# Two float32r passes in place of three bfloat16 passes for a feed-forward product, and V's columns packed

## The chip, the cores and the metric

The kernel runs on one core of a Trainium2 chip. The metric is device time in microseconds (us) for one execution, lower is better. The engines are named as in the profile: PE is TensorE's matmul (PEld its weight loads), DVE is VectorE, ACT is ScalarE, POOL is GpSimd, SP is the engine that issues the DMAs.

## The reference

Four sublayers in a row act on x of 16 batches × 256 tokens × 256 features in float32. After each one, its output is added to its input and a layer norm follows:

```python
x = layernorm(x + L0_attn(x))   # 16 heads; Fourier transform of q and kv per head, cumulative sum over tokens
x = layernorm(x + L0_ffn(x))    # gate over 8 experts, the best expert's low-rank update
x = layernorm(x + L1_attn(x))   # softmax attention, 16 heads of 16 features
x = layernorm(x + L1_ffn(x))
```

The change concerns the last two. In the last one the weights are ternary: each group of 64 is replaced by −1, 0 or 1 times a bfloat16 scale.

```python
w1 = ternary(W_fc)                       # 1024 x 256
h = square(relu(x @ w1.T))               # the product that is changed
h = h * rsqrt(mean(h*h) + eps)
out = h @ ternary(W_proj).T
```

In softmax attention, each head's 256 tokens × 16 features of V are multiplied by the exponentials of the scores. The sum of the exponentials comes from a column of ones beside V's 16 columns.

## The kernel before, in words

**Order of the work.** The kernel writes down operations with engines, planned costs, inputs, outputs and priorities. `Order.run` then goes through a planned time, picks at each step the operation that can start first (among those within a small slack, the one of the best priority) and emits it. The order on each engine is therefore fixed when the kernel is built, and it follows from the planned costs: `pe([pb], [xs, (w1T, q)], 12 * 0.11, go)` is one such cost. Where an operation lists two ways, such as ACT or DVE, the planner takes the one that ends first.

**Stages.** The 16 batches go in 4 groups of 4. `front(b)` computes the first two sublayers of one batch. `attention(i)` computes softmax attention for group i: products for Q, K and V (L810), a first pass of scores (L864) whose row maxima DVE reduces (L873), a second pass (L898) that ACT exponentiates (L907), products with V (L913), and the output product (L955). `back(b)` computes the last sublayer of one batch. While attention of group i has priority, `back` of group i−1 and `front` of group i+1 fill in. The `back` of the last group comes after everything else.

**The last sublayer, `back`.** PE transposes x3 to put features on partitions (L977). x is then split into an exact sum of three bfloat16 terms in tile `xs`: ACT copies and rounds the first (L980), DVE subtracts it into `rest` (L981), ACT or DVE rounds the second (L983), DVE or POOL subtracts for the third (L988, L989). For each of four `q`, PE computes 256 rows of h as 2 × 6 matmuls of 256 columns (L1000): two feature halves by three terms. ACT takes relu (L1009), ACT or DVE squares it (L1012, L1013), ACT squares again for the mean (L1017), and DVE or POOL sums that over the hidden features (L1025). L1035 is the second product, in float32; L1044 sums the squares over partitions; L1054 scales and adds x3; a layer norm follows. There are two `xs` buffers, one `h`, one `sq` and twelve `work` buffers.

**Weights.** `ternary` computes w1T (bfloat16) and w2T (float32) once in SBUF, with an eviction from PSUM at the end (`evacuate`, L359 on ACT or L360 on DVE).

**V.** Tile `v` holds, for each of 32 blocks of 128 tokens and 4 batches, 32 columns: 16 features, one column of ones, 15 columns of zeros. POOL sets it up with two memsets (L425, L426), and for each group four DMAs (L835) write the 16 features of one batch each from DRAM. L913 takes the 32 columns as the stationary operand, and the 32 result rows of each batch go to one quarter of PSUM's partitions. L921 to L925 use only the first 17.

Of the kernel before, what the change touches and what calls it, by code (L numbers as in the profile page):

```python
# [9 lines left out]

F32 = mybir.dt.float32
BF16 = mybir.dt.bfloat16
AF = mybir.ActivationFunctionType
ALU = mybir.AluOpType
AX = mybir.AxisListType
# [2 lines left out]
P = 128  # L18
D = 256
S = 256  # L20
NB = 16
GB = 4
NG = NB // GB
H = 16
HD = 16
NE = 8
NR = 8
HID = 1024
# [112 lines left out]
class Order:  # L141
# [11 lines left out]
    def fixed(self, ap):  # L153

        t = Logical(None, None, None)
        t.slot = Slot(ap)
        return t
# [126 lines left out]
def forward(ctx, tc, x, xt, wq, wkv, wo0T, f0, degen, cs, wqkvT, wo1T, wfc, wproj, cst, out):  # L284
# [5 lines left out]
    order = Order(tc)  # L290
# [3 lines left out]
    def place(name, shape, dtype=F32):  # L294
        return sb.tile(shape, dtype, name=name)

    def const(name, shape):
        return fixed(place(name, shape))
# [29 lines left out]
        order.slot("wb", place(f"wb{i}", [P, 512], BF16))  # L328
        order.slot("sb", place(f"sb{i}", [P, 8], BF16))
    for i in range(2):  # L330
        order.slot("xs", place(f"xs{i}", [P, 3 * 512], BF16))
    order.slot("lane", *[None] * 4)
    order.limit = {("ps", "r"): 2, ("ps", "a"): 6, ("lane", "r"): 2}
    v = const("v", [P, 2 * H, GB, 32])

    order.slot("vd", *[dp.tile([GB, S - VT, NJ * HD], F32, name=f"vd{i}") for i in range(2)])
    o = const("o", [P, S // 32, D])
# [51 lines left out]
    dg = const("dg", [72, D])  # L389
    slope, center = const("slope", [P, NE]), const("center", [P, NE])  # L390
    wqr, wo1 = const("wqr", [P, 2, 3 * D]), const("wo1", [P, 2, D])
    w1T, w2T = fixed(place("w1T", [P, 2, HID], BF16)), const("w2T", [P, HID // P, D])
    a = lambda t: t.slot.ap

    order.prio = -10.0
# [26 lines left out]

    dve([ones], [], P, lambda: V.memset(a(ones), 1.0))
    dve([mhalf], [], 2, lambda: V.memset(a(mhalf), -0.5))
    pool([v], [], 3.6, lambda: G.memset(a(v), 0.0))  # L425
    pool([v], [], 0.3, lambda: G.memset(a(v)[:, :, :, HD : HD + 1], 1.0))  # L426

    def warm():

# [370 lines left out]
    def attention(i):  # L800
# [32 lines left out]
        for g in range(GB):  # L833
            op(
                (SP, 0.1, lambda g=g: nc.sync.dma_start(  # L835
                    a(v)[:, :, g, 0:HD],
                    vd.slot.ap[g].rearrange("t e -> (t e)")[2 * ZQ * HD - VT * NJ * HD :].rearrange("(n p d) -> p n d", p=P, d=HD),
                )),
                [(v, g)], [vd],
            )  # L840
# [10 lines left out]
        def part(g, rows, which, h, at=0, n=S):  # L851
            lo = which * ZQ + h * S + at
            return zt_[32 * g : 32 * g + rows, lo : lo + n]


        for hh in range(2):
# [32 lines left out]
        for hp in range(H // 2):  # L889
            av = ps([P, 2, S], "a")  # L890
            for hk in range(2):
                h = hp * 2 + hk
                sc = [ps([P, 2, S], "a") for _ in range(GB)]

                def go(sc=sc, h=h):
                    for c in range(2):
                        for g in range(GB):
                            T.matmul(  # L898
                                sc[g].v[:, c, :], part(g, HD + 1, 1, h, c * P, P), part(g, HD + 1, 0, h),
                                start=True, stop=True,  # L900
                            )

                pe(sc, [zq, zr[h // 8], v, turn], 0.95, go, mode="r")
                es = []
                for g in range(GB):
                    e = tile_("es", [P, 2, S])
                    act([e], [sc[g]], 512, lambda e=e, sc=sc, g=g: A.activation(e.v, sc[g].v, AF.Exp, scale=HD ** -0.5))  # L907
                    es.append(e)

                def go(es=es, av=av, h=h, hk=hk):  # L910
                    for c in range(2):
                        for g in range(GB):
                            T.matmul(  # L913
                                av.v[32 * g : 32 * g + 32, hk, :], a(v)[:, h * 2 + c, g, :], es[g].v[:, c, :],
                                start=(c == 0), stop=(c == 1),
                            )

                pe([(av, hk)], [*es, v, turn], 0.87, go, mode="c")

            ou, rc = tile_("work", [P, 2, S // 32, 32]), stat(2, S // 32)  # L920
            dve([ou], [av], 512, lambda ou=ou, av=av: V.transpose(ou.v.rearrange("p k u d -> p (k u d)"), av.v.rearrange("p k s -> p (k s)")))  # L921
            dve([rc], [ou], 80, lambda ou=ou, rc=rc: V.reciprocal(rc.v.unsqueeze(3), ou.v[:, :, :, HD : HD + 1]), us=0.22)
            dve(
                [(o, hp)], [ou, rc], 256,
                lambda ou=ou, rc=rc, hp=hp: V.tensor_tensor(  # L925
                    a(o)[:, :, ts(hp, 2 * HD)].rearrange("p u (k d) -> p k u d", d=HD),
                    ou.v[:, :, :, 0:HD],
                    rc.v.unsqueeze(3).to_broadcast([P, 2, S // 32, HD]),
                    ALU.mult,
                ),  # L930
                us=0.42,
            )
# [33 lines left out]
    def back(b, late):  # L966
# [1 line left out]
        kind = "p" if late else "r"  # L968
        x3 = x3s.pop(b)

        xs, rest = tile_("xs", [P, 3, 2, S]), tile_("work", [P, 2, S])
        bx = ps([P, 2, S], kind)

        def go():
            for t in range(2):
# [2 lines left out]

        pe([bx], [x3, small, terned], 0.43, go)
        act([(xs, 0)], [bx], 512, lambda: A.copy(xs.v[:, 0], bx.v))  # L980
        dve([rest], [bx, (xs, 0)], 512, lambda: V.tensor_tensor(rest.v, bx.v, xs.v[:, 0], ALU.subtract))  # L981
        op(
            [(ACT, 0.57, lambda: A.copy(xs.v[:, 1], rest.v)), (DVE, 0.6, lambda: V.tensor_copy(xs.v[:, 1], rest.v))],  # L983
            [(xs, 1)], [rest],
        )
        op(
            [
                (DVE, 0.7, lambda: V.tensor_tensor(xs.v[:, 2], rest.v, xs.v[:, 1], ALU.subtract)),  # L988
                (POOL, 1.3, lambda: G.tensor_tensor(xs.v[:, 2], rest.v, xs.v[:, 1], ALU.subtract)),  # L989
            ],  # L990
            [(xs, 2)], [rest, (xs, 1)],
        )
        h, sq, acc = tile_("h", [P, HID // P, S]), tile_("sq", [P, HID // P, S]), tile_("work", [P, S])
        for q in range(HID // P // 2):
            pb = ps([P, 2, S], kind)

            def go(pb=pb, q=q):
                for i in range(2):
                    for n in range(6):
                        T.matmul(  # L1000
                            pb.v[:, i, :], a(w1T)[:, n // 3, ts(q * 2 + i, P)], xs.v[:, n % 3, n // 3, :],
                            start=(n == 0), stop=(n == 5),
                        )

            pe([pb], [xs, (w1T, q)], 12 * 0.11, go)
            r = tile_("work", [P, 2, S])
            hq = lambda q=q: h.v[:, q * 2 : q * 2 + 2, :]

            act([r], [pb], 512, lambda pb=pb, r=r: A.activation(r.v, pb.v, AF.Relu))  # L1009
            op(  # L1010
                [
                    (ACT, 0.57, lambda r=r, hq=hq: A.activation(hq(), r.v, AF.Square)),  # L1012
                    (DVE, 0.73, lambda r=r, hq=hq: V.tensor_tensor(hq(), r.v, r.v, ALU.mult)),  # L1013
                ],
                [(h, q)], [r],
            )
            act([(sq, q)], [(h, q)], 512, lambda hq=hq, q=q: A.activation(sq.v[:, q * 2 : q * 2 + 2, :], hq(), AF.Square))  # L1017
# [114 lines left out]
```

## Time and profile before

| | us |
|---|---|
| three runs: median (lowest to highest) | 840.29 (838.42 to 840.89) |
| the profiled execution's own time | 840.28 |
| its span from first to last instruction | 838.3 |
| PE busy | 801.0 |
| DVE busy | 636.5 |
| ACT busy | 433.9 |
| POOL busy | 118.1 |
| L1000: 768 matmuls, busy | 95.9 |
| L1000's weight loads, busy | 75.9 |

All profile numbers come from one execution. A busy time is the union of the durations of instructions; matmuls are pipelined, so a matmul's duration (282 ns on average at L1000) is longer than the distance to the next one, and the distance is what counts for throughput. Weight loads (PEld) overlap the matmuls before them. The granted clock of TensorE was 0.944 on average. Where a line of the profile ends in brackets, it gives idle time ahead of the instruction and the instruction that ended it. "L1000" is line 1000 of the kernel before.

### The profile page before, as it was taken

The page shows a single profiled execution, that of the slowest core. Times are in us where ns is not written, and L with a number is a line of the kernel's source. Part 1 is how long each engine was busy: PE and PEld are TensorE (multiplying, and loading weights), DVE is VectorE, ACT ScalarE, POOL GpSimd, SP SyncE. Part 2 cuts the span into 40 slices and gives each one's busy share as a digit, 9 for nine tenths or more (in the row PEclk, how much of TensorE's full clock was granted, in tenths as well). Part 3 has the DMA queues.
Part 4 walks back from the last instruction along what each step waited for, and adds up shares of the span by engine and source line. Part 5 has one row for each costly group of instructions (what it writes and reads, how often), then busy time and mean ns, then how long its engine had stood idle before and what let it go on. Part 6 is the DMA issues. An engine that isn't in the chain of part 4 may idle for free.

```text
span 838.3 us, 15181 instructions
## 1 busy us (share of the span) xinstructions
PE 801.0 (96%) x5912; PEld 568.5 (68%) x5912; DVE 636.5 (76%) x1442; ACT 433.9 (52%) x858; POOL 118.1 (14%) x309
## 2 busy tenths in 40 slices
PE   9997799999989999998999999999999999999896
PEld 6775468765665676775666676776566678856785
DVE  2888799766778998866579899767668898644654
ACT  5745410268762444676562444875752425395652
POOL 1022000010131011012012001112120001101212
PEclk9998695699999999999799999999999899999998
DMA  8001025000000431011000440000000610000000
GB/s 297 18 24 39 0 46 67 14 15 26 28 13 2 76 49 27 14 39 39 5 23 1 75 51 15 27 26 11 4 1 20 81 13 27 14 15 1 2 26 25
DMA packets 86892, 27.17 MB, mean 32 GB/s; under 512 B 67932, under 2 KB 84132, under 8 KB 86820
## 3 DMA queue, kind: packets, MB, share of 16 engines
q1 hardware_dynamic: 86820, 26.20, 14.4%
q8 instruction: 46, 0.75, 0.4%
q14 instruction: 26, 0.21, 0.1%
HBM read 16.76 MB, written 8.91 MB: 31 GB/s over the span
## 4 chain that ended last, share of the span: by engine, by line
PE 83%; DVE 8%; ACT 5%; POOL 1%; issue 1%; DMA 1%; DVEq 0%; ACTq 0%; POOLq 0%
PE bank L1035 11%; PE bank L1000 10%; PE bank L810 10%; PE bank L864 10%; PE bank L913 8%; PE bank L898 8%; PE bank L598 6%; PE bank L955 3%; PE bank L697 3%; DVE nm L873 2%; PE bank L721 2%; PE bank L643 2%; PE bank L782 2%; PE bank L544 2%; DVE work L1025 1%
## 5 line engine op out<-in xcount | busy, mean ns | idle before, releaser
L907 ACT ACTIVATE zt<-bank 128x512 f32<-128x512 f32 x256 | 135.6, 609 | 79.4 <-PE bank L898 79.0
L873 DVE TENSOR_REDUCE nm<-bank 128x2 f32<-128x512 f32 x256 | 157.2, 680 | 13.3 <-PE bank L864 13.1
L1035 PE MATMUL bank<-w2T,h 128*128 128x256 f32 x512 | 118.5, 383 | 0.0
L1035 PEld LDWEIGHTS bank<-w2T,h 128*128 128x128 f32 x512 | 94.5, 190 | 17.2 <-issue 5.6
L864 PE MATMUL bank<-zt 16*128 16x256 f32 x1024 | 99.8, 457 | 0.5 <-DVE nm L873 0.4
L552 POOL TENSOR_SCALAR st<-st 128x2 f32<-128x2 f32 x80 | 17.0, 213 | 580.2 <-DVE st L560 387.0
L1000 PE MATMUL bank<-xs,w1T 128*128 128x256 bf16 x768 | 95.9, 282 | 1.7 <-DVE xs L988 0.8
L1000 PEld LDWEIGHTS <-w1T 128*128 128x128 bf16 x768 | 75.9, 101 | 21.8 <-issue 10.4
L810 PE MATMUL bank<-wqr,x2T 128*128 128x512 f32 (+1 forms) x256 | 87.7, 499 | 0.9 <-ACT x2T L359 0.9
L864 PEld LDWEIGHTS bank<-zt 16*128 16x128 f32 x1024 | 68.2, 209 | 25.1 <-DVE nm L873 10.8
L898 PE MATMUL bank<-zt 17*128 17x256 f32 x1024 | 81.9, 417 | 0.6 <-ACT zt L907 0.4
L913 PE MATMUL bank<-zt,v 128*32 128x256 f32 x1024 | 78.7, 393 | 1.1 <-ACT zt L907 1.0
L810 PEld LDWEIGHTS bank<-wqr,x2T 128*128 128x128 f32 x256 | 49.1, 195 | 36.5 <-issue 30.4
L898 PEld LDWEIGHTS bank<-zt 17*128 17x128 f32 x1024 | 53.4, 192 | 24.7 <-issue 15.7
L819 DVE STREAM_TRANSPOSE zt<-bank 128x1024 f32<-128x1024 f32 (+1 forms) x48 | 64.5, 1455 | 5.9 <-PE bank L810 5.0
L1025 DVE TENSOR_REDUCE work<-sq 128x256 f32<-128x2048 f32 x16 | 59.0, 3688 | 3.9 <-ACT sq L1017 3.9
L598 PE MATMUL bank<-wf,x 128*128 128x512 f32 x128 | 61.3, 611 | 0.0
L1009 ACT ACTIVATE work<-bank 128x512 f32<-128x512 f32 x64 | 38.1, 598 | 43.7 <-PE bank L1000 35.7
L553 POOL TENSOR_TENSOR st<-st,mhalf 128x2 f32<-128x2 f32 x80 | 57.4, 718 | 6.2
L913 PEld LDWEIGHTS bank<-zt,v 128*32 128x32 f32 x1024 | 32.1, 110 | 36.4 <-ACT zt L907 11.8
L359 ACT COPY work<-bank 128x512 f32<-128x512 f32 (+1 forms) x33 | 16.9, 511 | 69.5 <-PE bank L810 65.3
L558 DVE BATCH_NORM_STATS2 st<-work 128x6 f32<-128x256 f32 x116 | 43.1, 412 | 0.4
(204 smaller groups left out, 1135.1 us busy)
## 6 DMA issues: line engine op xcount, KB each, us to landing
x<-in_xT SPq DMA_DIRECT2D x16, 256.0 KB
v<-vd SPq DMA_DIRECT2D x16, 256.0 KB
out<-work SPq DMA_DIRECT2D x16, 256.0 KB
x<-in_x SPq DMA_DIRECT2D x12, 256.0 KB
vd<-work SPq DMA_DIRECT2D x12, 256.0 KB
vd<-work SPq DMA_DIRECT2D x12, 128.0 KB
h<-in_wfc SPq DMA_DIRECT2D x4, 256.0 KB
sq<-in_wproj SPq DMA_DIRECT2D x4, 256.0 KB
```

Of the source, the lines that this page charges most:

```text
L553: pool([dst], [dst, mhalf], 0.7, lambda: G.tensor_tensor(dst.v, dst.v, a(mhalf)[:, 0:n], ALU.pow))
L598: T.matmul(pb.v.rearrange("p a s k -> p (a s k)"), xT.v[:, c, ts(t, P)], a(wf)[:, c].rearrange("p a s f -> p (a s f)"), start=(c == 0), st ...
L810: T.matmul(b.v.rearrange("p j d -> p (j d)"), x2T.v[:, c, tb].rearrange("p g k -> p (g k)"), a(wqr)[:, c, j0 * HD : (j0 + nj) * HD], start ...
L819: lambda b=b, tb=tb, j0=j0, nj=nj: V.transpose(ztv[:, j0 : j0 + nj, ts(tb, 32)], b.v.unsqueeze(2).to_broadcast([P, nj, 2, HD])),
L864: T.matmul(sc[g].v[:, t, :], part(g, HD, 0, h, t * P, P), part(g, HD, 1, h), start=True, stop=True,)
L873: lambda nm=nm, sc=sc, g=g, h=h: V.tensor_reduce(nm.v[:, g, h % 8, :], sc[g].v, AX.X, ALU.max, negate=True),
L898: T.matmul(sc[g].v[:, c, :], part(g, HD + 1, 1, h, c * P, P), part(g, HD + 1, 0, h), start=True, stop=True,)
L907: act([e], [sc[g]], 512, lambda e=e, sc=sc, g=g: A.activation(e.v, sc[g].v, AF.Exp, scale=HD ** -0.5))
L913: T.matmul(av.v[32 * g : 32 * g + 32, hk, :], a(v)[:, h * 2 + c, g, :], es[g].v[:, c, :], start=(c == 0), stop=(c == 1),)
L1000: T.matmul(pb.v[:, i, :], a(w1T)[:, n // 3, ts(q * 2 + i, P)], xs.v[:, n % 3, n // 3, :], start=(n == 0), stop=(n == 5),)
L1025: (DVE, 2.2, lambda: V.tensor_reduce(acc.v, sq.v.rearrange("p k s -> p s k"), AX.X, ALU.add)),
L1035: T.matmul(pw.v[:, t, :], h.v[:, k, ts(t, P)], a(w2T)[:, k, :], start=(k == 0), stop=(k == HID // P - 1))
```

## The change

The first product of `back` gets x as a sum of two float32 terms[...] held as float32r, in place of three bfloat16 terms. w1T is kept as float32r too. ACT's copy (L980) rounds the first term, DVE's subtraction (L981) leaves the second, and the later cast and subtraction go. A group of one `q` has 2 × 4 matmuls in place of 2 × 6, and its planned cost goes from 12 × 0.11 to 8 × 0.11. `xs` takes 4 KB per partition and buffer in place of 3 KB, and w1T 8 KB in place of 4 KB.

V's blocks are packed to 17 columns: 16 features and the column of ones. The matmul still takes 32 columns, so 15 of them are the features and ones of the blocks behind, and rows 17 to 31 of the result, which nothing uses, are no longer zero. One memset to 1.0 sets up the whole tile. The tile has 15 columns at its end so that the last slice stays inside.

```diff
-        order.slot("xs", place(f"xs{i}", [P, 3 * 512], BF16))
+        order.slot("xs", place(f"xs{i}", [P, 2 * 512], F32R))
-    v = const("v", [P, 2 * H, GB, 32])
+    v = const("v", [P, 2 * H * GB * (HD + 1) + 31 - HD])
-    w1T, w2T = fixed(place("w1T", [P, 2, HID], BF16)), const("w2T", [P, HID // P, D])
+    w1T, w2T = fixed(place("w1T", [P, 2, HID], F32R)), const("w2T", [P, HID // P, D])
-    pool([v], [], 3.6, lambda: G.memset(a(v), 0.0))
-    pool([v], [], 0.3, lambda: G.memset(a(v)[:, :, :, HD : HD + 1], 1.0))
+    va = a(v)[:, 0 : 2 * H * GB * (HD + 1)].rearrange("p (n g d) -> p n g d", g=GB, d=HD + 1)
+    pool([v], [], 2.0, lambda: G.memset(a(v), 1.0))
...
-                    a(v)[:, :, g, 0:HD],
+                    va[:, :, g, 0:HD],
...
+        def v_part(g, n):
+            at = (n * GB + g) * (HD + 1)
+            return a(v)[:, at : at + 32]
...
-                                av.v[32 * g : 32 * g + 32, hk, :], a(v)[:, h * 2 + c, g, :], es[g].v[:, c, :],
+                                av.v[32 * g : 32 * g + 32, hk, :], v_part(g, h * 2 + c), es[g].v[:, c, :],
...
-        xs, rest = tile_("xs", [P, 3, 2, S]), tile_("work", [P, 2, S])
+        xs = tile_("xs", [P, 2, 2, S])
...
-        dve([rest], [bx, (xs, 0)], 512, lambda: V.tensor_tensor(rest.v, bx.v, xs.v[:, 0], ALU.subtract))
-        op(
-            [(ACT, 0.57, lambda: A.copy(xs.v[:, 1], rest.v)), (DVE, 0.6, lambda: V.tensor_copy(xs.v[:, 1], rest.v))],
-            [(xs, 1)], [rest],
-        )
-        op(
-            [
-                (DVE, 0.7, lambda: V.tensor_tensor(xs.v[:, 2], rest.v, xs.v[:, 1], ALU.subtract)),
-                (POOL, 1.3, lambda: G.tensor_tensor(xs.v[:, 2], rest.v, xs.v[:, 1], ALU.subtract)),
-            ],
-            [(xs, 2)], [rest, (xs, 1)],
-        )
+        dve([(xs, 1)], [bx, (xs, 0)], 512, lambda: V.tensor_tensor(xs.v[:, 1], bx.v, xs.v[:, 0].bitcast(F32), ALU.subtract))
...
-                    for n in range(6):
+                    for n in range(4):
                         T.matmul(
-                            pb.v[:, i, :], a(w1T)[:, n // 3, ts(q * 2 + i, P)], xs.v[:, n % 3, n // 3, :],
-                            start=(n == 0), stop=(n == 5),
+                            pb.v[:, i, :], a(w1T)[:, n // 2, ts(q * 2 + i, P)], xs.v[:, n % 2, n // 2, :],
+                            start=(n == 0), stop=(n == 3),
                         )
-            pe([pb], [xs, (w1T, q)], 12 * 0.11, go)
+            pe([pb], [xs, (w1T, q)], 8 * 0.11, go)
```

## The prediction

> **What bounds the kernel now.** I read the page's busy times first, then its chain of work that ended last. In the first line each engine has busy time, share of the span and instructions; in the second, each entry is a line of the kernel with its share of the chain.
>
> ```profile
> PE 801.0 (96%) x5912; PEld 568.5 (68%) x5912; DVE 636.5 (76%) x1442; ACT 433.9 (52%) x858; POOL 118.1 (14%) x309
> PE bank L1035 11%; PE bank L1000 10%; PE bank L810 10%; PE bank L864 10%; PE bank L913 8%; PE bank L898 8%; PE bank L598 6%; PE bank L955 3%; PE bank L697 3%; DVE nm L873 2%; PE bank L721 2%; PE bank L643 2%; PE bank L782 2%; PE bank L544 2%; DVE work L1025 1%
> ```
>
> PE carries the chain, and L1000, the product that the change rewrites, is 10% of it (some 87 us). But an average over stages hides where another engine is level with PE. So next I cut the run at the stages of batch groups 1 to 3 (columns: window, its length, busy time of PE, PEld, DVE, ACT, POOL, granted clock, DMA share, GB/s).
>
> ```profile
> 276.00:325.00 49.00, 48.94 (x429) 36.55 (x429) 47.16 (x76) 16.81 (x29) 2.19 (x6) 1.00 0.33 48
> 325.00:440.00 115.00, 109.58 (x906) 76.73 (x905) 82.47 (x242) 78.60 (x159) 19.35 (x55) 0.96 0.09 27
> 465.00:520.00 55.00, 54.84 (x463) 40.85 (x460) 52.79 (x90) 20.48 (x39) 4.64 (x14) 0.97 0.33 49
> 520.00:620.00 100.00, 98.62 (x846) 66.76 (x844) 70.88 (x204) 72.98 (x152) 15.94 (x44) 1.00 0.05 15
> 648.00:700.00 52.00, 51.93 (x409) 37.21 (x409) 46.93 (x70) 18.23 (x32) 2.06 (x3) 0.90 0.31 41
> 700.00:775.00 75.00, 74.33 (x759) 53.38 (x753) 40.31 (x84) 47.94 (x92) 11.35 (x30) 1.00 0.05 16
> 775.00:838.30 63.30, 52.62 (x353) 46.07 (x351) 36.14 (x62) 30.74 (x55) 12.65 (x34) 0.95 0.05 18
> ```
>
> Two kinds alternate. In 276–325, 465–520 and 648–700 (first score pass, row maxima L873 on DVE) PE and DVE are both full. In 325–440, 520–620 and 700–775 (second score pass, exponentials) PE alone is full. Narrowed to L1000, each of these six windows holds 96 of its 768 matmuls, and the tail from 775 us holds 192. The timeline of a first pass shows the balance (start, duration, engine, line).
>
> ```profile
> 280.76 1.49 PE L1000 MATMUL bank<-xs,w1T 128*128 128x256 bf16 x12
> 280.91 8.70 DVE L873 TENSOR_REDUCE nm<-bank 128x2 f32<-128x512 f32 x14 [1.03 <-PE bank L864]
> 282.17 0.74 PEld L864 LDWEIGHTS bank<-zt 16*128 16x128 f32 x16 [0.21 <-issue]
> ```
>
> PE alternates a score group and an L1000 group: L1000 starts at 280.76 and again at 283.25, a period of 2.49 us. DVE does four maxima in the same time, 8.70/14 × 4 = 2.49 us. Neither waits.
>
> **What the skill says, against this trace.** "FP8 and Floating Point Precision", TensorE Precision Notes: true float32 takes four passes through the array, while reduced-precision float32 reads the four bytes and truncates. The trace agrees with the four: on the chain 48 bf16 matmuls of 256 columns took 5.24 us, 109 ns each; a float32 product at L1035 is two records, 24 of which took 5.18 us, so 2 × 216 = 432 ns, four times as long. No float32r runs here. One pass for it is my reading of that note.
>
> "TensorE: Matmul & The Clock Gate", Weight-path perf modes: fast weight load works for 128 columns if the dtype isn't FP32. The rows agree that float32 loads are slower.
>
> ```profile
> L1035 PEld LDWEIGHTS bank<-w2T,h 128*128 128x128 f32 x512 | 94.5, 190 | 17.2 <-issue 5.6
> L1000 PEld LDWEIGHTS <-w1T 128*128 128x128 bf16 x768 | 75.9, 101 | 21.8 <-issue 10.4
> 299.22 0.55 PEld L1044 LDWEIGHTS bank<-ones,work 128*128 128x128 f32 x4
> 774.93 0.60 PE L977 MATMUL bank<-small,x 128*128 128x128 f32 x4
> ```
>
> A mean duration is latency, though; what counts is how closely loads follow each other. Four float32 loads with one-column matmuls (L1044) took 0.55 us, so (550 − 192)/3 = 119 ns apart. Four float32 transposes (L977), each with its own load, took 0.60 us with one of 273 ns at the end, so 109 ns apart. A float32-sized load therefore fits about the 109 ns that a 256-column pass takes; it isn't the 190 ns of the row.
>
> **The change, part by part.**
>
> *L1000, removed.* There are 16 batches × 4 = 64 groups; each goes from 12 matmuls to 8. At one pass and 109 ns a group falls from 1.31 to 0.87 us: 64 × 4 × 0.109 = 27.9 us of PE. The records that ran at half clock take about twice that, which I don't count. By place:
> - Second-pass windows: 32 matmuls off in each, 3.5 us × 3 = 10.5. PE idles there 5.4 of 115, 1.4 of 100 and 0.7 of 75 us, so nearly all is real: I take 9.4 (90%).
> - First-pass windows: also 10.5 on PE, but a shorter L1000 group leaves DVE's 2.49 us period standing. DVE idles only 49.00 − 47.16 = 1.8, 2.2 and 5.1 us there, and loses of its own two third-term subtractions, 2 × 0.68 = 1.4 us. Each window can give between 1.4 (DVE's loss) and 3.5 us, unless the planner moves other PE work in. I take 2.1 each, 6.3.
> - Tail: 192 matmuls, of which the chain holds 176 (46, 12, 36, 12, 24 and 46). A third of 176 × 0.109 is 6.4 us.
>
> *The split of x.* One float32r copy on ACT (L980, 0.59 us) and one subtraction on DVE (L981, 0.68) stay, with a float32-sized output. The cast L983 (13 on ACT at 0.61, 3 on DVE) and the third term L988 (14 on DVE at 0.68, 2 on POOL) go. Mostly they lie beside PE work. In the tail they are on the chain (start, duration, step):
>
> ```profile
> 815.94 0.61 DVE work L981
> 816.55 0.02 issue
> 816.57 0.63 ACT xs L983
> 817.20 0.02 issue
> 817.22 0.70 DVE xs L988
> ```
>
> The last batch's L1000 starts right behind, at 817.96: 0.63 + 0.70 = 1.3 us off. The first tail batch has the same pair at 778.48–779.72: 1.2 off. Together 2.5 us. What is late next there is PE itself with L1035. One work buffer per batch is freed as well, priced at nothing, since the longest waits name none.
>
> *Costs taken at nothing.* Writing float32r instead of bf16: a 128x512 ACT copy took 586–590 ns with either output. w1T's four evictions likewise. V's packing: one POOL memset of 2191 columns for two of 4096 and 128; by the first (3.51 us) some 1.9 us instead of 3.8, with V first used at 153.6 us. Stationary slices of V stay 32 contiguous columns; now 15 of them hold neighbours' values that nothing reads. The load (L913) starts at multiples of 68 bytes; its 110 ns load hides behind 256-column streams, bound +10% of those loads, none exposed.
>
> *V's DMA.* 16 transfers of 64-byte pieces, destination step 68 instead of 128 bytes. The skill ("DMA: Bandwidth & Descriptors", How a descriptor splits into AXI transactions) says that pieces not starting at 256-byte steps begin at the boundary below, which costs beats; so some pieces may cost more. No such pieces run here. Lower bound 0; upper bound twice: the DMA share is 0.73–0.78 over the 15 us of each group's transfer, so up to 11.7 us later. V lands at about 143, 300, 490 and 673 us; the second pass starts at 153.6, 325.3, 518.5 and 703.0. Cover of 11 us or more; doubled, group 0's row-maxima transfers, queued behind V on SP (landed by 144), would come 2 us late. I take 0.
>
> *Sum:* 9.4 + 6.3 + 6.4 + 2.5 = 24.6 us. The profiled run took 840.28 us (span 838.3 plus 2.0 around it), 0.01 from the median of 840.29. 840.3 − 24.6 = 815.7. No wait is added. The planner writes a new order of all work from the shorter costs; I allow ±6 us for where fillers now fall.
>
> **The rivals.**
>
> *A, slower: float32r isn't one pass.* If the array takes four-byte moving data at half rate, a matmul costs what one float32 record of 256 columns does, 216 ns. Float32 transposes of 128 columns take 109 ns, the price of 256 bf16 columns, which speaks for it; that transposes needn't be paced like products speaks against, as does the skill's note. Then L1000 costs 512 × 216 = 110.6 against 83.9 us: +26.7 us on PE, less 2.5 from the split: 864 us. It decides above 83.9/512 = 164 ns per matmul; at 140 ns, a float32 load's duration as a floor, half the gain stays: about 828.
>
> *B, DVE keeps the first passes.* One pass, but the first-pass windows give only 1.4 us each (4.2) and the tail's third-to-fourth gap absorbs half of its 8.9: 840.3 − 9.4 − 4.2 − 4.4 = 822. PE that waits more could also fall to half clock, as it did in 123–155 us (0.54 granted while DVE was full), which the skill (the same TensorE page, Part 1: The HAM clock gate) ascribes to idle windows of 3.4 us; two such windows would add about 3: 825.
>
> *C, more than the sum.* Before the last split, PE idles 808.7–817.9 while L1025 (3.7 us) holds DVE. A shorter split may be placed ahead of it: up to 6 us more, 809.
>
> **How the numbers follow.** One pass near the sum 0.50; B 0.25; C 0.10; A 0.15, of which the 140 ns middle case 0.02 and the slow one 0.13. The predicted time is the likeliest, 816. The first three cases lie in 803–830; the slow one's 864 would need a range that no case fills in between, so I stop at 834 and leave it out, with a little more for a worse order. The fast cases and the middle one hold 0.87; I give 0.03 of it to a worse order that eats the gain down to within 0.3% (2.5 us, about what a measurement of this kernel can tell from no change): faster 0.84, same 0.03, slower 0.13.
>
> **What would show it.** L1000 with 512 records of 108–120 ns from start to start, in groups of eight of about 0.9 us; PE busy about 770–775 us; no L983 or L988; second-pass windows shorter by 3 us each with PE still full; first-pass windows shorter by 1.4–3.5 us, DVE over 96% busy and PE with gaps. V landing at least 5 us before each second pass. The prediction is wrong if L1000's spacing is over 164 ns, if PE idles tens of us more at half clock, or if the second passes begin by waiting on V.

## The result: no change beyond the noise

| | us |
|---|---|
| before, median of 20 runs (lowest to highest) | 839.46 (838.15 to 840.89) |
| after, median of 20 runs (lowest to highest) | 839.17 (833.69 to 841.2) |
| ratio after to before, 95% interval | 0.9991 (0.998 to 1.0002) |
| the profiled execution after, and its span | 840.1, 838.3 |
| mean granted clock, before and after | 0.944, 0.92 |

The prediction said 816. The product got shorter, by rather less than it said; the larger part of the gain was lost elsewhere. In the kernel after, line numbers are a few off: L994 is the product (L1000 before), L985 and L986 are ACT's copy and DVE's subtraction of the split, L1029 is the second product (L1035), L869 the first pass of scores (L864), L878 its row maxima (L873), L903 the second pass (L898).

The page after, engine totals and chain, as shown for before:

```profile
PE 803.6 (96%) x5656; PEld 575.5 (69%) x5656; DVE 632.8 (75%) x1428; ACT 420.8 (50%) x842; POOL 114.7 (14%) x306
PE bank L1029 12%; PE bank L869 12%; PE bank L811 10%; PE bank L903 8%; PE bank L918 8%; PE bank L994 8%; PE bank L599 6%; DVE nm L878 3%; PE bank L698 3%; PE bank L960 2%; PE bank L722 2%; PE bank L644 2%; PE bank L783 2%; PE bank L545 2%; DVE st L559 1%; PE bank L662 1%
```

There are 256 matmuls fewer (5912 to 5656), and L994's share of the chain fell from 10% to 8%. Yet PE's busy time rose, from 801.0 to 803.6 us, and L869, which the change doesn't touch, went from 10% to 12%. The product itself is close to a single pass (first the chain: start, duration, step; then the groups by line and form: busy time, mean ns of one, idle time before):

```profile
339.43 2.83 PE bank L994 x24
```

```profile
L869 PE MATMUL bank<-zt 16*128 16x256 f32 x1024 | 117.3, 505 | 1.3 <-DVE nm L878 1.3
L994 PE MATMUL bank<-xs,w1T 128*128 128x256 f32 x512 | 72.5, 294 | 1.2 <-DVE xs L986 1.2
```

24 matmuls in 2.83 us are 118 ns each. From start to start inside a group, at full clock, the median step is 118 ns (363 of 372 steps lie between 115 and 122), against 109 for bfloat16. L869's busy time was 99.8 us before: 17.5 us more for the same 1024 matmuls.

In every trace here the granted clock is either 1.00 or 0.50, and a number between is the mean of a window. A stretch at 0.50 is called half clock below; most steps of the product took 213 ns in such stretches, in before as in after.

The windows of before, cut again (window, length, busy PE, PEld, DVE, ACT, POOL with counts, granted clock, DMA share, GB/s):

```profile
276.00:325.00 49.00, 48.29 (x366) 35.17 (x368) 44.08 (x74) 9.67 (x18) 3.10 (x8) 0.93 0.49 51
325.00:440.00 115.00, 111.48 (x904) 76.42 (x897) 85.22 (x239) 81.99 (x168) 19.82 (x56) 0.97 0.09 27
465.00:520.00 55.00, 54.70 (x406) 37.97 (x406) 49.89 (x87) 16.41 (x34) 4.80 (x11) 0.88 0.42 50
520.00:620.00 100.00, 98.71 (x813) 72.00 (x811) 71.16 (x195) 67.98 (x139) 17.71 (x46) 0.95 0.04 12
648.00:700.00 52.00, 52.00 (x359) 37.37 (x358) 47.27 (x75) 12.26 (x23) 2.20 (x6) 0.77 0.44 51
700.00:775.00 75.00, 74.11 (x733) 54.19 (x733) 36.14 (x63) 52.09 (x101) 6.96 (x18) 0.98 0.04 12
775.00:838.30 63.30, 53.93 (x322) 49.02 (x320) 39.11 (x72) 28.99 (x54) 14.89 (x40) 0.96 0.05 17
```

Read the first, third and fifth. PE is "busy" throughout, but with fewer matmuls than before (366, 406 and 359, where there were 429, 463 and 409) and at a lower clock (0.93, 0.88, 0.77 for 1.00, 0.97, 0.90). ACT shows the same: 9.67, 16.41 and 12.26 us for 16.81, 20.48 and 18.23. The fillers of `back` have left the first passes. The stage times, each from the first matmul of a kind to the first of the next, say where the time went:

| us against before | predicted | after |
|---|---|---|
| up to group 1's first QKV matmul | 0 | +1.6 |
| QKV to first second-pass score, groups 1 to 3 | −6.3 | +3.5 −3.2 −5.5 = −5.2 |
| first second-pass score to next QKV or output product | −9.4 | −7.2 +10.9 +7.0 = +10.7 |
| tail from the last group's output product | −8.9 | −7.1 |
| sum | −24.6 | 0.0 |

The second passes, where PE alone is full and 9.4 us were to be gained, got 10.7 longer: that is where the fillers went. The timeline of group 2's and group 3's first passes shows one step of how they were pushed out (start, duration, engine, line):

```profile
491.05 0.59 ACT L985 CAST xs<-bank 128x512 fp32r<-128x512 f32 x1 [0.18 <-PE bank L982]
...
493.24 2.46 DVE L878 TENSOR_REDUCE nm<-bank 128x2 f32<-128x512 f32 x4
...
515.34 0.66 DVE L986 TENSOR_TENSOR xs<-bank,xs 128x512 fp32r<-128x512 f32 x1
...
683.04 0.59 ACT L985 CAST xs<-bank 128x512 fp32r<-128x512 f32 x1 [3.21 <-PE bank L982]
...
698.37 0.68 DVE L986 TENSOR_TENSOR xs<-bank,xs 128x512 fp32r<-128x512 f32 x1
```

ACT rounded the first term at 491.05, and DVE subtracted at 515.34, 24.3 us later, with row maxima in between; in group 3 from 683.04 to 698.37, 15.3 us. The longest such distance in these passes before was 14.5 us. The L994 groups of that batch need the second term. So in group 2 one batch's product starts inside the first pass, and the next at 517.5, in the second pass, while before both started inside (473.6 and 496.5). In group 3 the second one starts at 699.4, 3.7 us before the first pass ends.

### The profile page after: what moved, and what is told of

Its sections match the earlier page's. It is cut to its first block, busy times and chain, and to the rows that moved or that the text cites. A ratio compares the mean times of both kernels' runs of the same rounds, so it can differ in the third digit from the quotient of the medians.

```text
span 838.3 us, 14648 instructions
## 1 busy us (share of the span) xinstructions
PE 803.6 (96%) x5656; PEld 575.5 (69%) x5656; DVE 632.8 (75%) x1428; ACT 420.8 (50%) x842; POOL 114.7 (14%) x306
## 4 chain that ended last, share of the span: by engine, by line
PE 83%; DVE 9%; ACT 5%; POOL 2%; issue 1%; DVEq 0%; ACTq 0%; POOLq 0%
PE bank L1029 12%; PE bank L869 12%; PE bank L811 10%; PE bank L903 8%; PE bank L918 8%; PE bank L994 8%; PE bank L599 6%; DVE nm L878 3%; PE bank L698 3%; PE bank L960 2%; PE bank L722 2%; PE bank L644 2%; PE bank L783 2%; PE bank L545 2%; DVE st L559 1%; PE bank L662 1%
## 5 line engine op out<-in xcount | busy, mean ns | idle before, releaser
L878 DVE TENSOR_REDUCE nm<-bank 128x2 f32<-128x512 f32 x256 | 157.3, 680 | 14.8 <-PE bank L869 14.4
L869 PE MATMUL bank<-zt 16*128 16x256 f32 x1024 | 117.3, 505 | 1.3 <-DVE nm L878 1.3
L1029 PE MATMUL bank<-w2T,h 128*128 128x256 f32 x512 | 118.1, 382 | 0.0
L1029 PEld LDWEIGHTS bank<-w2T,h 128*128 128x128 f32 x512 | 94.5, 190 | 16.4 <-issue 4.4
L869 PEld LDWEIGHTS bank<-zt 16*128 16x128 f32 x1024 | 81.9, 232 | 31.0 <-DVE nm L878 13.4
L903 PE MATMUL bank<-zt 17*128 17x256 f32 x1024 | 86.5, 422 | 1.8 <-ACT zt L912 1.6
L903 PEld LDWEIGHTS bank<-zt 17*128 17x128 f32 x1024 | 56.7, 195 | 25.8 <-issue 14.6
L994 PE MATMUL bank<-xs,w1T 128*128 128x256 f32 x512 | 72.5, 294 | 1.2 <-DVE xs L986 1.2
L994 PEld LDWEIGHTS bank<-xs,w1T 128*128 128x128 f32 x512 | 64.9, 193 | 9.2 <-issue 3.4
L360 ACT COPY work<-bank 128x512 f32<-128x512 f32 (+1 forms) x29 | 14.5, 500 | 62.4 <-PE bank L811 61.3
```

Of the source, the lines that this page charges most:

```text
L869: T.matmul(sc[g].v[:, t, :], part(g, HD, 0, h, t * P, P), part(g, HD, 1, h), start=True, stop=True,)
L878: lambda nm=nm, sc=sc, g=g, h=h: V.tensor_reduce(nm.v[:, g, h % 8, :], sc[g].v, AX.X, ALU.max, negate=True),
L903: T.matmul(sc[g].v[:, c, :], part(g, HD + 1, 1, h, c * P, P), part(g, HD + 1, 0, h), start=True, stop=True,)
L994: T.matmul(pb.v[:, i, :], a(w1T)[:, n // 2, ts(q * 2 + i, P)], xs.v[:, n % 2, n // 2, :], start=(n == 0), stop=(n == 3),)
L1029: T.matmul(pw.v[:, t, :], h.v[:, k, ts(t, P)], a(w2T)[:, k, :], start=(k == 0), stop=(k == HID // P - 1))
```

## The experiments

Ratios are to the kernel before, with 95% intervals. "Old instructions" are the three bfloat16 terms, "new" the two float32r ones. Two explanations stood against each other, and the expectations call them theories. The order theory: the planner's new order took the gain. The clock theory: float32r, or less bfloat16 work, brings half clock in any order, and this took it. Code is cut where a diff has "...".

**Is it the order or the instructions?** x_old_order runs the new instructions in the old order: planned with the old costs, and with two empty operations where the planner had the cast and the third subtraction.

```diff
-    pool([v], [], 2.0, lambda: G.memset(a(v), 1.0))
+    pool([v], [], 3.6, lambda: G.memset(a(v), 1.0))
+    pool([v], [], 0.3, lambda: None)
...
-        dve([(xs, 1)], [bx, (xs, 0)], 512, <the subtraction, written to xs.v[:, 1]>)
+        dve([rest], [bx, (xs, 0)], 512, <the same subtraction, written to xs.v[:, 1]>)
+        op([(ACT, 0.57, lambda: None), (DVE, 0.6, lambda: None)], [(xs, 1)], [rest])
+        op([(DVE, 0.7, lambda: None), (POOL, 1.3, lambda: None)], [(xs, 2)], [rest, (xs, 1)])
...
-            pe([pb], [xs, (w1T, q)], 8 * 0.11, go)
+            pe([pb], [xs, (w1T, q)], 12 * 0.11, go)
```

> The new instructions in the old order: float32r split and product, V packed, but the planner is given the old cost (12 x 0.11) and the old two operations of the split as empty ones, so every remaining instruction stands where it stood before. Order theory (the new order, which leaves the second batch's subtraction behind the row maxima on DVE, eats the gain): L1000's group falls from 1.31 to some 0.95 us, 64 x 0.36 = 23 us on PE, about three quarters of it real, plus up to 2.5 us in the tail: 818 to 824 us, granted clock 0.94 or more. Clock theory (float32r itself, or less bf16 work, brings the half clock in any order): clock 0.92 again and 834 to 840 us.

Measured: 823.02 us, 0.983 (0.9794 to 0.9867). Lined up by source line, the sequence of matmul groups on PE is that of before from end to end. So by the medians the instructions are worth 839.5 − 823.0 = 16.5 us in that order, and the order that the planner wrote for them costs 839.2 − 823.0 = 16.2. The two cancel. Two of the six runs took 830.6 and 831.3 us, at a granted clock of 0.934 where the other four had 0.946; by the ratio, which counts them, the instructions are worth 14 us (11 to 17). Whether the shorter cost of the product or the two missing operations set off the new order wasn't tried.

y_new_order is the reverse: the old instructions in the order of after. The three DVE operations of the split stand as one block where after has its subtraction, so casts that ran on ACT move to DVE too. The diff is against the kernel after; xs, w1T and the six matmuls are bfloat16 again.

```diff
+        def split():
+            V.tensor_tensor(rest(), bx.v, term(0), ALU.subtract)
+            V.tensor_copy(term(1), rest())
+            V.tensor_tensor(term(2), rest(), term(1), ALU.subtract)
-        dve([(xs, 1)], [bx, (xs, 0)], 512, <the one subtraction>)
+        dve([(xs, 1)], [bx, (xs, 0)], 512, split)
...
             pe([pb], [xs, (w1T, q)], 8 * 0.11, go)
```

> The old instructions in the new order: three bfloat16 terms (one copy on ACT; subtraction, rounding and second subtraction in one block on DVE, 1.8 us), 12 matmuls per group, but planned as the changed kernel is; V packed. Order theory: the order of the changed kernel with 23 us more PE work and 16 x 1.1 us more DVE work: 852 to 866 us. Clock theory: the clock returns to 0.944 as the bf16 work fills PE again, and the time is within 4 us of 840.

Measured: 866.22 us, 1.0318 (1.0289 to 1.0347), at the far edge of what was expected. The sequence of matmul groups on PE is that of after from end to end. In this order the old instructions are 26.7 us slower than in their own, part of which may be the extra work on DVE. From here to after the instructions gain 27.0. The clock theory fits neither run: one kernel with float32r took 823 us, and one without it 866.

**How much is float32r's own step?** bf2 keeps the order of after, and holds the two terms as bfloat16.

```diff
-        order.slot("xs", place(f"xs{i}", [P, 2 * 512], F32R))
+        order.slot("xs", place(f"xs{i}", [P, 2 * 512], BF16))
...
-    w1T, w2T = fixed(place("w1T", [P, 2, HID], F32R)), const("w2T", [P, HID // P, D])
+    w1T, w2T = fixed(place("w1T", [P, 2, HID], BF16)), const("w2T", [P, HID // P, D])
```

> The changed kernel with bfloat16 in place of float32r for both terms and for w1T: the third term of x is left out of the product, so h is less exact; order and instruction counts are those of the changed kernel. Order theory: only the spacing of 119 ns falls to 109, 512 x 10 ns = 5 us, most of it real: 834 to 837 us, clock still about 0.92, L986 still late. Clock theory (float32r draws the half clock): clock 0.944 and 815 to 822 us.

Measured: 832.87 us, 0.9932 (0.991 to 0.9955), 6.3 us under after by the medians and a little faster than expected. Start to start its product takes 109 ns at full clock where after has 118; 512 × 9 ns is 4.6 us. One group behind a group of scores in each kernel, after first, then bf2 (start, duration, engine, line), shows that the distance isn't all:

```profile
298.65 1.22 PE L994 MATMUL bank<-xs,w1T 128*128 128x256 f32 x8
```

```profile
299.58 1.05 PE L994 MATMUL bank<-xs,w1T 128*128 128x256 bf16 x8
```

Behind other work, the second matmul of a float32r group starts late: of 33 such groups at full clock in after, 26 have a first step of 201 to 232 ns and 7 a longer one, while in bf2 30 of 32 have 108 to 120. Behind another group of the same product it is 115 to 122 in 28 of 29. Some 0.1 us for each of 33 groups is 3.3 us, so an estimate from both is 7.9 us on PE. The weight loads, from each kernel's list for this line (count: shortest, median, longest ns, first and last start), after first, then bf2:

```profile
L994 PEld LDWEIGHTS bank<-xs,w1T x512: 186/188/333, 250.7 to 822.7; 128*128 128x128 f32 x171
```

```profile
L994 PEld LDWEIGHTS <-w1T x512: 95/98/181, 247.1 to 815.1; 128*128 128x128 bf16 x171
```

A float32r load takes 188 ns, a bfloat16 one 98. At half clock the product's step is 213 ns in both formats (14 of 15 steps in after take 213 or 214, and 43 of 45 in before), so what float32r adds isn't a further pass of the array. The longer load is the likely reason for the 118 ns and for the late second matmul, which was argued from these durations and not tested. Either way it can't explain 16 us.

**V's packing** alone, in the kernel before: the hunks of the diff that touch `v`, and nothing else.

> The kernel before with V's columns packed and nothing else; planned costs and so the order are those of before. All theories: within 2 us of before. If pieces of 64 bytes at 68-byte steps cost more, the DMA share in the 15 us of each transfer of V rises over 0.73 to 0.78, hidden ahead of the second pass. If the packing itself costs what float32r gains: slower by 10 us or more.

Measured: 839.17 us, 0.9999 (0.9988 to 1.001). What stays is visible in the two transfer windows, first of before, then of vpack (columns as in the windows above):

```profile
130.00:145.00 15.00, 15.00 (x102) 12.03 (x98) 14.67 (x26) 0.26 (x1) 0.00 (x0) 0.50 0.74 74
475.00:490.00 15.00, 15.00 (x124) 11.44 (x126) 13.26 (x20) 9.38 (x19) 1.31 (x4) 0.92 0.78 85
```

```profile
130.00:145.00 15.00, 15.00 (x103) 12.05 (x101) 14.67 (x26) 0.26 (x1) 0.00 (x0) 0.50 0.98 74
475.00:490.00 15.00, 15.00 (x128) 11.29 (x126) 13.26 (x21) 9.38 (x19) 1.32 (x4) 0.95 1.03 76
```

The DMA engines' share rises from 0.74 and 0.78 to 0.98 and 1.03 for no more bytes, and PE and DVE do the same work. The mean 64-byte packet takes 14.5 ns in place of 10.5 (the median is 11 in both).

**What is it in the order?** The first theory was the late subtraction itself. split_first lets it go ahead of the row maxima (L986 alone).

```diff
-        dve([(xs, 1)], [bx, (xs, 0)], 512, <subtraction>)
+        dve([(xs, 1)], [bx, (xs, 0)], 512, <subtraction>, prio=order.prio - 20.0)
```

> The changed kernel with one number different: the subtraction that leaves the second term gets a priority ahead of the row maxima (order.prio - 20). Order theory: the second batch of each first pass starts its product some 16 to 20 us earlier, PE is filled again, clock back to 0.94: 820 to 828 us. Clock theory: clock stays near 0.92, 836 to 842 us.

Measured: 837.05 us, 0.996 (0.9947 to 0.9973): a miss, where the clock theory had put it. The gaps between copy and subtraction fell to 3.3 us at most in the first passes of groups 2 and 3, and they filled again, but almost nothing was gained.

The second theory was the half clock. warm puts four float32 matmuls of ones (4 × 0.22 us on PE) ahead of the last eight of the sixteen score groups in groups 2 and 3.

```diff
                 def go(sc=sc, h=h):
+                    if i > 1 and h > 7:
+                        for n in range(4):
+                            T.matmul(sc[0].v[:, 0, 0:P], a(ones), a(ones), start=True, stop=True)
```

> The changed kernel in its own order, with four extra float32 matmuls of ones (128x128x128, 0.87 us) ahead of each score group in the second half of the first pass of batch groups 2 and 3, where the changed kernel runs score groups alone at half clock; they write a bank that the scores then overwrite. Order theory: the half clock there is a symptom of PE having nothing to fill in; the granted clock rises to 0.94 but the time stays, 836 to 845 us. Clock theory: with the clock back the gain appears, 820 to 828 us.

Measured: 831.32 us, 0.9904 (0.987 to 0.9938): 7.9 us under after, between the two expectations. The first passes of groups 2 and 3, each from its first score to the first of the second pass: after, then warm.

```profile
461.90:513.20 51.30, 51.07 (x370) 35.76 (x369) 46.56 (x79) 12.25 (x23) 3.48 (x7) 0.87 0.46 55
652.80:703.10 50.30, 50.30 (x359) 37.78 (x358) 45.55 (x74) 11.81 (x21) 2.20 (x6) 0.73 0.44 50
```

```profile
455.80:507.90 52.10, 52.10 (x434) 39.53 (x433) 46.47 (x79) 12.25 (x23) 3.48 (x7) 0.97 0.47 58
643.50:691.20 47.70, 47.70 (x426) 37.30 (x425) 44.17 (x73) 11.41 (x21) 2.20 (x6) 0.96 0.48 52
```

The clock rises from 0.87 and 0.73 to 0.97 and 0.96, with 16 × 0.87 = 13.9 us of matmuls added, and the two passes stay as long as they were within 2.6 us. From its QKV product to its second pass, the first edited group became 0.9 us longer and the other 2.6 shorter. The profiled execution gained 12.1 us, but only this 1.7 where the edit stands: 6.2 fell ahead of the first edited group, where the two kernels are alike, and 4.2 in the second passes behind. So full clock in the first passes, bought with work of no use, brings almost nothing; what it would bring without that work this run doesn't show. The five runs lie between 827.8 and 837.0 us.

**More of `back` in the first passes.** The third theory was that all of `back`'s work on DVE must come ahead of the row maxima, and the planned cost must be what a group really takes. boost does both.

```diff
-  <L986 split, L1007 square, L1019 sum of squares, L1042 copy, L1048 scale and add>
+  <the same>, prio=order.prio - 20.0
...
-            pe([pb], [xs, (w1T, q)], 8 * 0.11, go)
+            pe([pb], [xs, (w1T, q)], 8 * 0.119, go)
```

> The changed kernel with two edits to the planner's input: back's DVE work up to the scaling (split, square, sum of squares, copy of the mean, scale and add) gets order.prio - 20, ahead of the row maxima, and L1000's group its measured cost, 8 x 0.119. Order theory, with starvation on DVE as its mechanism: two batches' last sublayer fit each first pass, 25 us or more of other PE work in each, time 812 to 824 us. If starvation isn't what the order lost: 830 to 842 us.

Measured: 809.71 us, 0.9654 (0.9633 to 0.9676): the fastest of all, 29.5 us under after with the same matmuls and the same other work, a few choices of the planner between ACT, DVE and POOL apart. The same two first passes, first in x_old_order, then in boost:

```profile
460.20:513.50 53.30, 52.95 (x429) 41.15 (x428) 50.23 (x82) 19.48 (x37) 5.10 (x12) 0.97 0.50 52
641.10:694.70 53.60, 53.60 (x414) 41.30 (x413) 48.45 (x75) 17.08 (x30) 1.97 (x5) 0.90 0.38 42
```

```profile
458.60:515.90 57.30, 56.86 (x475) 43.29 (x474) 54.97 (x93) 24.48 (x48) 4.60 (x13) 1.00 0.48 53
635.90:699.80 63.90, 63.89 (x527) 50.85 (x526) 59.97 (x96) 29.07 (x54) 5.30 (x14) 1.00 0.35 43
```

Matmuls in the passes go from 370 and 359 (after) to 429 and 414, and to 475 and 527, and the clock from 0.87 and 0.73 to 0.97 and 0.90, and to 1.00. The passes grow, from 51.3 and 50.3 us to 57.3 and 63.9, by less than the work they take in.

Is it then just a better order, whatever the instructions? before_boost gives the kernel before the same priority on DVE (by 11), and y_boost runs the old instructions in boost's order.

```diff
# before_boost, in the kernel before
-  <L981, L983, L988 split, L1013 square, L1025 sum of squares, L1048 copy, L1054 scale and add>
+  <the same>, prio=order.prio - 11.0
# y_boost, in boost
+  <split() and six matmuls as in y_new_order>
```

> Control: the kernel before with the same DVE operations of back (and the bfloat16 split's) at order.prio - 11. In the kernel before, two batches' last sublayer already stand in each first pass, so ahead of the row maxima they gain nothing: 838 to 846 us. If the priority by itself is worth the gain, 815 to 830 us.

Measured: 851.38 us (841.88 to 853.8), 1.0103 (1.0054 to 1.0152), slower than both expectations. It isn't a recipe: with these instructions the planner makes a slower order of it.

> The old instructions (three bfloat16 terms, split in one block on DVE, 12 matmuls per group) in the order of boost, V packed. If the instructions of the change are worth what the step-by-step sum said wherever PE is kept full, this stands 22 to 30 us above boost: 832 to 840 us. If the gain of boost is the order's alone: 812 to 822 us.

Measured: 843.05 us, 1.0056 (1.0028 to 1.0084), beyond the expected range. The sequence of matmul groups is that of boost. In the order that suits them the new instructions are worth 843.0 − 809.7 = 33.3 us, with the caveat that the old ones have all their casts on DVE here.

Which half of boost does it? cost_only takes the planned cost alone, prio_only the priorities alone.

```diff
# cost_only, in after
-            pe([pb], [xs, (w1T, q)], 8 * 0.11, go)
+            pe([pb], [xs, (w1T, q)], 8 * 0.119, go)
# prio_only, in boost
-            pe([pb], [xs, (w1T, q)], 8 * 0.119, go)
+            pe([pb], [xs, (w1T, q)], 8 * 0.11, go)
```

> The changed kernel with only the planned cost of L1000's group set to 8 x 0.119, no priority changed. Order theory with starvation on DVE: the row maxima still come first, so the first passes stay poor in other PE work: 834 to 846 us. If the wrong cost in the planner was what lost the gain: 808 to 824 us.

Measured: 852.86 us, 1.0151 (1.0135 to 1.0166), slower than both expectations.

> The changed kernel with only the priorities of boost, the planned cost left at 8 x 0.11. Order theory: most of boost's gain, first passes full: 812 to 826 us. If the priority does nothing by itself: 834 to 842 us.

Measured: 828.65 us, 0.9864 (0.9849 to 0.9878), between the two. The priorities gain 10.5 us on after and the cost loses 13.7; together they gain 29.5. The planner's answer isn't a sum of its inputs: 8% on one cost of PE moves the time by 13.7 us up or 18.9 down.

**One more at the clock.** boost_warm0 adds warm's four matmuls to boost in group 0, most of whose first pass stands at half clock in after and in boost.

```diff
+                    if i == 0:
+                        <four matmuls of ones, as in warm>
```

> boost, and in the first pass of batch group 0, which has no last sublayer to fill in, four extra float32 matmuls of ones (128x128x128) ahead of each score group, into a bank that the scores overwrite. There the score groups ran alone at half clock, 2.68 us per head, while DVE's four maxima take 2.49, and the half clock lasted some 9 us into the second pass. If the half clock has a price of its own, as warm suggests: 16 x 0.19 = 3 us and up to 4 us of the second pass, 803 to 807 us. If the extra work costs what it saves: 809 to 813 us.

Measured: 815.81 us (807.47 to 817.65), 0.9695 (0.9662 to 0.9728): not faster than boost, and past both expectations. Group 0's first pass, boost, then boost_warm0:

```profile
114.50:153.50 39.00, 38.59 (x278) 30.37 (x279) 38.21 (x69) 2.18 (x5) 0.00 (x0) 0.64 0.51 60
```

```profile
115.50:155.50 40.00, 39.33 (x397) 30.90 (x398) 37.13 (x65) 1.81 (x4) 0.00 (x0) 1.00 0.59 58
```

The clock goes from 0.64 to 1.00, and the pass from 39.0 to 40.0 us. In boost DVE was busy for 38.21 of the 39.00 us, so at most 0.8 us was there to gain while the row maxima stay. Here DVE is busy for less, 37.13 of 40.00, as PE now has the added matmuls to do. Where DVE has hardly any idle time to give, a faster PE buys next to nothing.

**What carries the differences.** The table takes the three first passes of groups 1 to 3 together. "Other PE work" is every matmul in them but the scores, each counted at its line's full-clock distance (109 ns for the first product in bfloat16 and 117 in float32r, 216 for float32 of 256 columns, and so on), so it is an estimate from the traces. What is left of the length is scores, waits and half clock. Half clock is given for the whole run, and for the part of it between group 0's first pass and the tail that lies outside these passes, mostly in the second passes.

| kernel | length | other PE work | left | half clock, whole run | half clock, outside | median |
|---|---|---|---|---|---|---|
| boost | 186.5 | 117.1 | 69.4 | 83.5 | 32.2 | 809.7 |
| x_old_order | 158.0 | 77.5 | 80.5 | 90.6 | 28.7 | 823.0 |
| prio_only | 189.1 | 116.6 | 72.5 | 101.0 | 45.4 | 828.7 |
| split_first | 171.7 | 85.9 | 85.8 | 125.0 | 42.5 | 837.1 |
| after | 155.0 | 59.5 | 95.5 | 136.8 | 36.3 | 839.2 |
| cost_only | 159.5 | 59.6 | 99.9 | 154.7 | 47.2 | 852.9 |
| before (old instructions) | 162.4 | 86.4 | 76.0 | 96.8 | 29.1 | 839.5 |

In after, the passes are only 3.0 us shorter than in x_old_order with 18.0 us less work in them: 15.0 of the 16.2 us between the two. boost has 57.6 us more work in passes 31.5 us longer, 26.1 of its 29.5. For these two the column "left" holds nearly the whole difference. For the others it doesn't: split_first should be 9.7 us under after and is 2.1, prio_only 23.0 and is 10.5, cost_only 4.4 over and is 13.7 over. They lose another 8 to 13 us outside these passes. Half clock there is longer than in after by 6.2, 9.1 and 10.9 us. A step of the product took 213 ns at half clock and 109 or 118 at full, so that a half-clock stretch costs at most about half of its length. This makes at most 3.1, 4.6 and 5.5 us of it; what takes the rest isn't settled.

In the table's kernels with the new instructions, the time goes with half clock in the whole run, so the order could do its harm through half clock. From after to boost it falls by 53.3 us, half of which would be 26.7. But 47.4 of it lie in these first passes, where DVE leaves little to gain: in after it is busy for 47.78 of 53.40, 46.56 of 51.30 and 45.55 of 50.30 us, so with DVE's work as it is full clock could bring at most 15.1. Outside, after has 4.1 us more than boost, worth at most 2. And warm has less half clock than boost, 76.8 us, and takes 21.6 us more with 13.9 us of added matmuls. So half clock alone can't be the 29.5 us. How much of the loss goes through it isn't settled.

## Why the prediction was wrong

**The step that failed** is one sentence: "The planner writes a new order of all work from the shorter costs; I allow ±6 us for where fillers now fall." The order cost 16 us, the whole gain of x_old_order, and other orders of the same instructions lie between 809.7 and 852.9, a spread of 43 us against the allowed 12. The prediction did name "a worse order that eats the gain", but gave it a chance of 0.03 and no mechanism. It should have been a case of its own with a place and a size. The place could be read from the profile: in the first passes PE and DVE were both full at a period of 2.49 us, so each us of `back` that leaves them must come back in a second pass, where PE is full and nothing hides it. The way out of them was there too, since the split's DVE step stands behind row maxima of better priority.

**Why the shorter product set it off.** The planner gives DVE to the row maxima whenever one is ready, as they belong to attention. That a product group of planned 0.88 in place of 1.32 us brings the next four maxima earlier, so that DVE is offered one at each turn and `back` doesn't get in, fits the distances of 15.3 and 24.3 us and the priorities' gain of 10.5 us in prio_only. split_first shows that the subtraction is not the only such step. That the earlier row maxima are the planner's reason was argued, not shown.

**The mis-sized terms.** x_old_order has the order that the sum assumed, so its stages can be set against it.

| us | predicted | x_old_order |
|---|---|---|
| first-pass stages, groups 1 to 3 | −6.3 | −1.0 −1.1 −2.3 = −4.4 |
| second-pass stages | −9.4 | −2.3 −1.0 −2.5 = −5.8 |
| tail, split included | −8.9 | −6.2 |
| start | 0 | −0.6 |
| sum | −24.6 | −17.0 |

The three predicted sizes are 1.4 to 1.6 times those measured. Part of it is the distance of the matmuls. The prediction worked out 119 ns from L1044's loads and 109 from the float32 transposes, and took the lower: 118 was measured. With it the product saves 64 × (1308 − 944) ns = 23.3 us of PE rather than 27.9. The late second matmul behind other work takes some 0.1 us more from about half of the groups (34 of 57 at full clock in x_old_order), 3.4 us or a little over. That leaves about 20 us, and 27.9 is 1.4 times as much. bf2 puts the two together at 6.3 us by its median. What is still missing in the second passes wasn't taken apart.

**What was right.** What bounds each stage: 18.0 us of other PE work left the first passes from x_old_order to after, and the second passes got 16.5 us longer. One pass per float32r matmul, as the prediction read the note on float32 of reduced precision: 118 ns for 256 columns, a quarter of float32's 432 and a little over. Rival A, 216 ns, is out. V's DMA: packets took 14.5 ns in vpack and 15.7 in after where before had 10.5, 1.4 and 1.5 times as much, under the bound of twice. The Trainium skill ("DMA: Bandwidth & Descriptors", How a descriptor splits into AXI transactions) says that a transaction starts at a 256-byte boundary, and that the bytes between the boundary and the start of a piece cost beats too. That fits, but pieces at 128-byte steps can't all start on such a boundary either, and which pieces got slower wasn't looked at. Each of V's transfers took at most 2 us longer, and in after V landed 9.9 us or more before each second pass, hidden as taken.

**The rivals.** B named both things that went wrong, DVE keeping the first passes and PE falling to half clock there, but as small ones: "two such windows would add about 3". Half clock grew by 136.8 − 96.8 = 40.0 us, and B had no term for work that is pushed out. In C the last split did come earlier (the last batch's product starts at 811.8, not 817.5), but the tail got only 7.1 us shorter, so it wasn't worth 6 more on top of 8.9.

**The signs given.** "PE busy about 770–775" was 803.6, and the sign that was meant to warn, "if PE idles tens of us more at half clock", needed another word: PE didn't idle by the profile, it was busy at half clock.

## What to carry to other kernels

Where a planner or scheduler reads the costs of a change, test the instructions and the order apart: plan the new instructions with the old costs, and the old ones with the new costs. Here that showed some 16 us gained and 16 lost behind a result of nothing, and the way to a version 3.5% faster than before. When a stage has two full engines and its neighbours have one, look at which work stands in it as filler, and at the one instruction that lets the filler in.

## What the runs showed of the hardware

**A PE that the profile calls busy can be held at half clock.** In after, two stretches where score groups ran nearly alone (first two lines after, then the same times in boost, where other work stands between):

```profile
495.30:509.00 13.70, 13.70 (x62) 8.58 (x64) 11.59 (x22) 1.77 (x4) 1.31 (x4) 0.50 0.13 38
676.20:703.50 27.30, 27.30 (x159) 20.19 (x161) 24.45 (x44) 4.04 (x8) 2.00 (x5) 0.50 0.32 26
```

```profile
495.30:509.00 13.70, 13.26 (x110) 8.45 (x112) 13.69 (x25) 3.20 (x10) 1.30 (x3) 1.00 0.06 20
676.20:703.50 27.30, 27.29 (x217) 21.49 (x213) 25.02 (x40) 15.76 (x30) 3.50 (x10) 1.00 0.04 11
```

PE's busy time says 13.70 of 13.70 and 27.30 of 27.30 us, at a clock of 0.50. The Trainium skill ("TensorE: Matmul & The Clock Gate", Part 1: The HAM clock gate) puts the half clock down to idle windows of 3.4 us. The stretches here are 13.7 and 27.3 us, about four and eight of those, but in neither does the profile draw PE idle at all. So its busy time can't tell whether the clock will be granted; what the gate counts these runs don't show. With four float32 matmuls of 128 × 128 × 128 per score group in warm, the two passes had 0.97 and 0.96.

**Runs of one kernel can differ with the clock that they were granted.** Of boost_warm0's six runs, one took 807.47 us at a mean clock of 0.976 and five 815.5 to 817.7 at 0.962 to 0.964; of x_old_order's, four took 821.6 to 823.1 at 0.946 and two 830.6 and 831.3 at 0.934. What decides it from run to run wasn't tried.

**float32r costs a little more than its pass:** 118 ns between matmuls of 256 columns with their loads of 188 ns, where bfloat16 has 109 and 98; and mostly 201 to 232 ns for the first step of a group behind other work, where bfloat16 has 108 to 120. At half clock both take 213.
